# A four-stage attention, routing and expert kernel on one core: the first loads and keys reordered, and the first late expert job's rows fetched and transposed earlier

## The chip, the core and the metric

The kernel runs on one core of a Trainium2 chip. The core has five engines with their own instruction queues: TensorE (PE, with its weight loads shown apart as PEld), VectorE (DVE), ScalarE (ACT), GpSimd (POOL) and SyncE (SP, which here only issues DMAs). They are tied together by semaphores. The metric is the device time of one execution in microseconds (us). Before the change three runs took 1174.27, 1172.83 and 1172.62 us, median 1172.83. One further execution was profiled; all durations in this document that come from a trace come from such a profiled execution.

## The reference

Input `x` has 8 batches of 512 tokens of 256 numbers; a context of 64 rows per batch is attended to. All in 32-bit floats.

```
x = x + attention0(layernorm(x), ctx, ctx)        # 16 heads of 16, 64 keys per batch
x = x + ffn(layernorm(x))                         # in each batch the 75% of tokens
                                                  # with the highest score get gelu(x @ w_block)
x = x + attention1(layernorm(x), ctx, ctx, mask)
x = x + moe(x)                                    # 8 experts, the 2 best of each token, weights
                                                  # renormalised: silu(x@g) * (x@u) @ down, inner width 1024
```

The keys and values of both attentions depend only on the context and the weights, not on `x`. Which tokens go to which expert is known only once the third stage of all batches is done.

## The kernel before

**Two phases.** In the front phase (to about 545 us) the eight batches pass through both attentions, the feed-forward and the routing. The routing writes each token's row, 260 numbers wide with its token number, experts and weights behind the 256 features, into a DRAM buffer `xs` sorted by expert, with indirect scatters on GpSimd (L864). In the second phase the experts run as "jobs". A full job is 256 rows of one expert: fetch the rows, transpose them (4 matmuls against the identity), a gate-and-up product of 8 chunks of 8 matmuls each, the silu by ScalarE and two products on VectorE, 32 matmuls of outputs, a scaling by the routing weight on VectorE, and an indirect add of the rows to the output in DRAM on GpSimd (L106). Smaller jobs ("one", "pair") handle what is left over.

**Early and late jobs.** Seven full jobs (`NEARLY`) are early: they are put between the steps of the front phase as soon as half the batches are routed, with weights in buffers of their own (`e_wgu`, `e_wdn`). `early_steps(j)` gives their loads and their steps: `enter` (transposes L1159, copy L1162, token numbers and weights L1164 to L1176), four `gates` of two chunks each (matmuls L1183, activation L1191, products L1192 and L1193), and two `down` (matmuls L1210, scaling L1218, add). The other jobs follow in `order`, each with `load` (SP: two register loads, rows L1325, gate weights L1348, down weights L1354), `enter` (transposes L1365, copy L1367, token numbers and weights L1371 to L1385), `gate_up_full` (L1397, L1405, L1406) and `down` (L1454, L1462). A job's outputs are put behind the gates of the job after it. The first late job's list comes from `full_list`, on VectorE, which ends in writing `jobs`. Its rows may be fetched once the last scatter has landed (`routed`).

**Order.** Within an engine the order of the front phase is written out by hand in the string `ORDER`. Each letter takes the next step of one chain: a digit is a batch, A to H a batch's rank work, `k` keys, `v` values of one batch for both layers, `s` set-up steps sorted by a due time, `l` the two job lists, `j` early jobs. `in_order` ties the steps on PE, DVE, ACT and POOL to each other; SP's DMAs have no part in it and go in program order.

**The start.** SP, ScalarE and POOL issue the first loads in program order. `first_keys` makes layer 0's keys (L354) in two chunks and spreads each by ScalarE into a block-diagonal form `kbd` with a bias (L363, biased by `bkh`, which POOL makes at L349). `keys(1, c)` does the same for layer 1 on PE (L372) and VectorE (L380). `batch_values` makes one batch's values (L392), which VectorE biases and spreads into `vbd` (L401). A batch's attention is: statistics (L433 to L436), the reciprocal deviation `rstd` on POOL (L438), `shift` (L444), normalised rows `xn` (L447), transposes (L462) and copies (L465), queries (L494, L501), scores `sc` (L524), their maxima (L531, `pm` L539), scores the other way round and the exponentials (L547 to L564), context (L576), denominators `pz` (L591) and `bz` (L606), the product (L614), output projection (L625). The statistics step of batch 2 is in `ORDER` ahead of the shift step of batch 1.

Of the kernel before, what the change touches and what calls it, by code (L numbers as in the profile page):

```python
# [8 lines left out]
F32 = mybir.dt.float32  # L9
I32 = mybir.dt.int32  # L10
AF = mybir.ActivationFunctionType
# [4 lines left out]
P = 128  # L16
# [11 lines left out]
E = 8  # L28
# [19 lines left out]
NQ = P // QR  # L48

ORDER = """  # L50
sssssssssss0k0vvv0ss1020001s0k110s1s0s031010s7s2s403202410030v20120ss01040502A010A30A0As
101013010343201130005s12010sk0112151761Bs2B1BB112120241201v102s2050223s022302412C22123C2
C021C02131012110323150030sv024110331231041025231052000043313234260000D14D34Ds14D2341v233
613421632333442123454126154343114325134311114432E2524E1111544E452356E5472243423725234653
5264345645256352452222F36F35F63F222246455635547335546357453674356647435356733333556646v7
l63333476G464jj77j5jGj666j5j7jj47Gjjj765j7457j4G5j64654j7j6556747j5j7644644444j76sH6jj56
4444j557j76j7j57jj7Hsj76jjjjHH7565j65jj676jj7jj6j57j5j6j75557j5555jj7j6j667j55557jjjs67j
66j76j7676j66j76s66667j7jjjj7jj6666j77j7j7jjjjj77jjs7j7j7j7j7j777jj77jjjljj77jj77jj
"""


# [1 line left out]
def xattn_ffn_kernel(ctx: ExitStack, tc: tile.TileContext, a: dict, out: bass.AP):  # L63
# [53 lines left out]
    with ExitStack() as front:  # L117
# [49 lines left out]
        for t in range(TB):  # L167
            q = (nc.scalar, nc.scalar, nc.sync, nc.sync)[t]
            q.dma_start(x_sb[:, t, :], x_t[0][:, t, :])
        load_layer(0, ("wv", "wq"), nc.sync)  # L170
        nc.sync.dma_start(x_sb[:, TB : 2 * TB, :], x_t[1])
        load_layer(0, ("bo", "wo"), nc.sync)
        load_layer(1, ("wk", "bk"), nc.sync)
        for b in range(2, 4):
            nc.sync.dma_start(x_sb[:, b * TB : (b + 1) * TB, :], x_t[b])
        w_block = load_mat(nc.sync, "w_block")
# [55 lines left out]
        mhalf = const.tile([P, TB], F32, name="mhalf")  # L232
        setups.append((-0.9, lambda: nc.gpsimd.memset(mhalf, -0.5)))

        def loaded():
            load_layer(0, ("bk",), nc.gpsimd)
            load_layer(1, ("wv",), nc.gpsimd)

        setups.append((-0.862, loaded))

        def loaded():
            for l in range(2):
                load_layer(l, ("bv",), nc.gpsimd)
            load_layer(0, ("bq",), nc.gpsimd)

        setups.append((-0.855, loaded))

        ownh = within(
            -0.88, "ownh", [HC],
# [89 lines left out]
            layers[l]["vbd"] = vbd[:, l]  # L339
        setups.append((-0.93, lambda: nc.vector.memset(vbd[:, 0], 0.0)))  # L340
        setups.append((-0.858, lambda: nc.gpsimd.memset(vbd[:, 1], 0.0)))
        bkh = const.tile([P, 2, NC], F32, name="bkh")

        def first_keys():

            w = layers[0]
            two = [ps_m.tile([P, B, SK], F32, tag="m", name=f"ps_k_0_{c}") for c in range(NC)]
            for i in range(2):
                nc.gpsimd.tensor_scalar(  # L349
                    bkh[:, i, :], w["bk"], headm[:, i : i + 1], None, ALU.mult  # L350
                )
            for k in range(NC):
                for c in range(NC):
                    nc.tensor.matmul(  # L354
                        two[c],
                        lhsT=w["wk"][:, k, c * P : (c + 1) * P],
                        rhs=ctxT[:, k],
                        start=(k == 0),
                        stop=(k == NC - 1),
                    )  # L360
            for c in range(NC):
                for i in range(2):
                    nc.scalar.activation(  # L363
                        w["kbd"][:, c, :, i, :], two[c], AF.Identity,
                        bias=bkh[:, i, c : c + 1], scale=headm[:, i : i + 1],
                    )

        def keys(l, c):
            w = layers[l]
# [737 lines left out]
        e_xg = part_of_room(2, RW)  # L1107
        e_xT = part_of_room(NC, 2, P)
        e_sg = [part_of_room(1, 2 * P)]
        e_now = keep.tile([P, 2, D], F32, name="e_now")  # L1110
        e_w = {}
        piece = 2 * P

# [118 lines left out]
        for b in range(B):  # L1232
# [2 lines left out]
                attention_steps(b, 0, layers[0], False) + ffn  # L1235
                + attention_steps(b, 2, layers[1], True) + route_steps(b)
            )
        chains["k"] = [first_keys] + [lambda c=c: keys(1, c) for c in range(NC)]
        chains["v"] = [lambda b=b: batch_values(b) for b in range(B)]
        chains["s"] = [step for _, step in sorted(setups, key=lambda p: p[0])]  # L1240
        chains["l"] = [early_list, full_list]
        chains["j"] = early = []
        jobs_steps = [early_steps(j) for j in range(NEARLY)]
        early += jobs_steps[0][0]
        for j, (_, steps) in enumerate(jobs_steps):

            loads = list(jobs_steps[j + 1][0]) if j + 1 < NEARLY else []
            for n, step in enumerate(steps):
                early.append(step)
                if loads and n != len(steps) - 2:  # L1250
                    early.append(loads.pop(0))


        engines = (
# [46 lines left out]
    def kind(j):  # L1301
        return "full" if j < NLATE else "one" if j < NLATE + NONE else "pair"

    def load(j, late=False):
# [16 lines left out]
        xg = moe.tile([P, 2, RW], F32, tag="xg", name=f"xg_{j}", bufs=3)  # L1321

        def rows():
            for u, (row, _) in enumerate(at):
                i = nc.sync.dma_start(  # L1325
                    xg[u * size : u * size + size, 0:subs, :],
                    xs[bass.ds(row, subs * size), :].rearrange("(s p) w -> p s w", p=size),
                ).ins

                if what == "pair":  # L1330
                    after(i, tail_sent)
                else:
                    for other in tail_sent:
                        tc.declare_no_dep(i, other, reason="rows of tokens alone")
                    after(i, routed)

        if not late:
            rows()
# [12 lines left out]
        if late:  # L1351
            rows()
# [131 lines left out]
    assert sorted(order) == [j for j in range(NJOB) if j != spare]  # L1484

    def load_at(i):
        return load(order[i], i == 0) if i < len(order) else None

    loads = [load_at(0), load_at(1)]
    entered = []  # L1490
    in_order(lambda: entered.append(enter(order[0], loads[0][0])))

    def placed(i, step):

        if i < NPIN:
            got = []
            in_order(lambda: got.append(step()))
            return got[0]
        return step()

    pending = None
    for i, j in enumerate(order):
        w = loads.pop(0)[1]
        xT, tok, wt = entered.pop(0)
        if i > 0:
            loads.append(load_at(i + 2))
        if i == 0:

            hT = placed(i, lambda: gate_up_full(j, xT, w, None, range(NF // 2)))
            entered.append(placed(i, lambda: enter(order[1], loads[0][0])))  # L1510
            placed(i, lambda: gate_up_full(j, xT, w, hT, range(NF // 2, NF)))
        elif j < NLATE:
            hT = placed(i, lambda: gate_up_full(j, xT, w))
        else:
            h, hT = placed(i, lambda: gate_up_rows(j, xT, w))
        if i == 0:
            small_list()
            unit_list()
            loads.append(load_at(2))
        if 0 < i < len(order) - 1:  # L1520
            entered.append(placed(i, lambda: enter(order[i + 1], loads[0][0])))
        if pending is not None:
            placed(i, lambda: down(*pending))
        if j >= NLATE:
            placed(i, lambda: turn(j, h, hT))
        pending = (j, hT, w, tok, wt)
# [55 lines left out]
```

## Time and profile before

| | before |
|---|---|
| median of three runs | 1172.83 us |
| the profiled execution | 1164.97 us |
| its span, first to last instruction | 1163.3 us |
| TensorE clock granted in it | 0.999 |
| PE busy | 1144.1 us |
| DVE, ACT, POOL busy | 571.8, 375.7, 285.1 us |
| moved by DMA | 203.5 MB, mean 175 GB/s |

The span lies 1.7 us below the execution's own time; the profiled execution lies 7.9 us below the median of the runs. A line of the timeline gives the start (us from the span's start), the duration (of several instructions in a row together), engine, line of the kernel, operation, what it writes and reads, how many, and in brackets how long its engine was idle before it and which instruction ended that idle time. "SPq" is the queue that issues DMAs; the duration there is that of the issue, not of the transfer.

### The profile page before, as it was taken

The page shows a single profiled execution, that of the slowest core. Times are in us where ns is not written, and L with a number is a line of the kernel's source. Part 1 is how long each engine was busy: PE and PEld are TensorE (multiplying, and loading weights), DVE is VectorE, ACT ScalarE, POOL GpSimd, SP SyncE. Part 2 cuts the span into 40 slices and gives each one's busy share as a digit, 9 for nine tenths or more (in the row PEclk, how much of TensorE's full clock was granted, in tenths as well). Part 3 has the DMA queues.
Part 4 walks back from the last instruction along what each step waited for, and adds up shares of the span by engine and source line. Part 5 has one row for each costly group of instructions (what it writes and reads, how often), then busy time and mean ns, then how long its engine had stood idle before and what let it go on. Part 6 is the DMA issues. An engine that isn't in the chain of part 4 may idle for free. (4 is left out here: it accounts for less than half of the span.)

```text
span 1163.3 us, 20921 instructions
## 1 busy us (share of the span) xinstructions
PE 1144.1 (98%) x8016; PEld 823.8 (71%) x8016; DVE 571.8 (49%) x1660; ACT 375.7 (32%) x717; POOL 285.1 (25%) x312
## 2 busy tenths in 40 slices
PE   8999999999999999999999999999999999999997
PEld 4556666656667778778887776777767777667886
DVE  6798888898877766555722221222222221222221
ACT  4655655645544342322222112121121211211210
POOL 6330134233340512332411212112121121211112
PEclk9999999999999999999999999999999999999999
DMA  9000001010134444355889689997798977986711
GB/s 271 3 1 2 1 20 39 19 57 20 38 119 137 128 128 134 108 160 156 265 331 341 218 282 300 322 307 226 265 310 312 315 235 269 307 313 228 277 15 19
DMA packets 119589, 203.53 MB, mean 175 GB/s; under 512 B 10401, under 2 KB 105249, under 8 KB 107969
## 3 DMA queue, kind: packets, MB, share of 16 engines
q1 hardware_dynamic: 100048, 179.35, 44.0%
q0 software_dynamic: 14640, 18.12, 7.7%
q10 hardware_dynamic: 4800, 4.72, 1.2%
q8 instruction: 64, 1.05, 0.4%
q14 instruction: 37, 0.30, 0.1%
HBM read 180.38 MB, written 23.47 MB: 175 GB/s over the span
## 5 line engine op out<-in xcount | busy, mean ns | idle before, releaser
L1397 PE MATMUL gu<-xjT,wgu 128*128 128x256 f32 x1152 | 252.0, 379 | 0.7 <-ACT xjT L1367 0.7
L1397 PEld LDWEIGHTS gu<-xjT,wgu 128*128 128x128 f32 x1152 | 217.6, 190 | 31.0 <-issue 1.2
L106 POOL DMA_INDIRECT out_dram<-now,tok x63 | 98.1, 1557 | 475.7 <-DVE now L1462 287.1
L1454 PE MATMUL o<-wdn,hT 128*128 128x256 f32 (+1 forms) x1008 | 189.2, 380 | 0.0
L1454 PEld LDWEIGHTS o<-wdn,hT 128*128 128x128 f32 (+1 forms) x1008 | 151.1, 173 | 28.3 <-issue 1.7
L1406 DVE TENSOR_TENSOR hT<-sg,gu 128x256 f32<-128x256 f32 x144 | 60.6, 421 | 189.4 <-ACT sg L1405 189.2
L1405 ACT ACTIVATE sg<-gu 128x256 f32<-128x256 f32 x144 | 55.3, 384 | 208.5 <-PE gu L1397 207.1
L1424 PE MATMUL gr<-wgu,xjT 128*64 128x512 f32 (+1 forms) x432 | 120.8, 596 | 0.0
L1183 PE MATMUL gu_e<-x_sb,e_wgu 128*128 128x256 f32 x448 | 101.6, 382 | 0.6 <-ACT x_sb L1162 0.6
L1183 PEld LDWEIGHTS gu_e<-x_sb,e_wgu 128*128 128x128 f32 x448 | 83.8, 190 | 15.6 <-issue 2.2
L1462 DVE TENSOR_SCALAR now<-o,wt 128x256 f32<-128x256 f32 x53 | 25.6, 483 | 139.1 <-PE o L1454 139.0
L1424 PEld LDWEIGHTS gr<-wgu,xjT 128*64 128x64 f32 (+1 forms) x432 | 42.8, 150 | 68.4 <-issue 66.9
L864 POOL DMA_INDIRECT xs<-xr,slots x64 | 63.2, 988 | 104.7 <-issue 35.4
L438 POOL TENSOR_TENSOR rstd<-ve,mhalf 128x4 f32<-128x4 f32 x32 | 33.0, 1030 | 223.3 <-DVE ve L436 177.8
L531 DVE TENSOR_REDUCE mx<-sc 128x32 f32<-128x2048 f32 x32 | 73.2, 2288 | 14.9 <-PE sc L524 14.6
L1434 DVE TENSOR_TENSOR h<-sg,gr 128x512 f32<-128x512 f32 x34 | 23.4, 688 | 82.9 <-PE gr L1424 82.8
L494 PE MATMUL ps_q<-xT,w_wq 128*128 128x512 f32 x128 | 62.0, 612 | 0.5 <-ACT xT L465 0.5
L1433 ACT ACTIVATE sg<-gr 128x512 f32<-128x512 f32 x34 | 20.3, 597 | 124.7 <-PE gr L1424 124.7
L625 PE MATMUL py<-w_wo,cT 128*128 128x256 f32 x256 | 60.3, 384 | 0.0
L625 PEld LDWEIGHTS py<-w_wo,cT 128*128 128x128 f32 x256 | 47.3, 190 | 11.6 <-issue 5.3
L447 ACT ACTIVATE xn<-x_sb,shift,rstd 128x256 f32<-128x256 f32 x96 | 49.8, 594 | 11.6 <-DVE shift L444 11.5
L433 DVE BATCH_NORM_STATS2 st<-x_sb 128x6 f32<-128x256 f32 x128 | 51.3, 400 | 3.6 <-DMA x_sb<-in_x_dram 3.6
(295 smaller groups left out, 1452.9 us busy)
## 6 DMA issues: line engine op xcount, KB each, us to landing
wgu<-in_guT_dram SPq DMA_DIRECT2D x90, 1024.0 KB, 9.7
wdn<-in_dnT_dram SPq DMA_DIRECT2D x45, 1024.0 KB, 6.0
e_wgu<-in_guT_dram SPq DMA_DIRECT2D x56, 256.0 KB, 3.6
e_wdn<-in_dnT_dram SPq DMA_DIRECT2D x7, 1024.0 KB, 6.0
xg<-xs SPq DMA_DIRECT2D x18, 260.0 KB, 7.2
out_dram<-x_sb ACTq DMA_DIRECT2D x8, 512.0 KB, 4.6
x_sb<-in_x_dram SPq DMA_DIRECT2D x7, 512.0 KB, 8.2
x_sb<-xs SPq DMA_DIRECT2D x7, 260.0 KB, 2.8
```

Of the source, the lines that this page charges most:

```text
L106: i = nc.gpsimd.indirect_dma_start(out=out_rows, out_offset=bass.IndirectOffsetOnAxis(ap=tok, axis=0), in_=rows, in_offset=None, bounds_ch ...
L433: nc.vector.bn_stats(st, x_sb[:, b * TB + t, :])
L494: nc.tensor.matmul(ps, lhsT=w["wq"][:, k, c * P : (c + 1) * P], rhs=got["xT"][:, k, :], start=(k == 0), stop=(k == NC - 1),)
L531: nc.vector.tensor_reduce(got["mx"].rearrange("p t (r h) -> p r t h", r=NQ)[:, :, :, 2 * c : 2 * c + 2], sc, AX.X, ALU.max,)
L625: nc.tensor.matmul(py[:, s, :], lhsT=cT[:, c, t * P : (t + 1) * P], rhs=w["wo"][:, c, :], start=(c == 0), stop=(c == NC - 1),)
L864: i = nc.gpsimd.indirect_dma_start(out=xs, out_offset=bass.IndirectOffsetOnAxis(ap=slots[:, t, k : k + 1], axis=0), in_=xr[:, t, :], in_of ...
L1183: nc.tensor.matmul(ps[:, half, :], lhsT=e_w["gu"][:, c, o : o + P], rhs=e_xT[:, c].rearrange("p s q -> p (s q)"), start=(c == 0), stop=(c ...
L1397: nc.tensor.matmul(ps[:, half, :], lhsT=wgu[:, c, o : o + P], rhs=xT[:, c].rearrange("p s q -> p (s q)"), start=(c == 0), stop=(c == NC - 1),)
L1405: nc.scalar.activation(sg[:, 0 : 2 * P], ps[:, 0, :], AF.Silu)
L1406: nc.vector.tensor_tensor(hT[:, f, :], sg[:, 0 : 2 * P], ps[:, 1, :], ALU.mult)
L1424: nc.tensor.matmul(ps[rows], lhsT=xT[:, c, 0, rows], rhs=wgu[:, c, o : o + 4 * P], start=(c == 0), stop=(c == NC - 1),)
L1454: nc.tensor.matmul(ps[rows], lhsT=hT[:, f, s * P + rows.start : s * P + rows.stop], rhs=wdn[:, f, :], start=(f == 0), stop=(f == NF - 1),)
```

## The change

- **Loads at the start.** SP loads layer 1's key weights first, then layer 0's query weights, batch 1, and after it both layers' value weights. Before, layer 0's value and query weights came first, and layer 1's value weights went by POOL's queue. Layer 1's key bias goes from SP's queue to POOL's. POOL issues layer 0's key bias first of all, then its query bias and layer 1's key bias, and the value biases after the first `rstd`.
- **Keys and values at the start.** `bkh` becomes a set-up step of its own. ScalarE's two spreads of layer 0's keys become two steps (`first_taken`), of which the second stands behind batch 0's copies. Layer 1's first keys take the place of the first three value products, directly behind layer 0's keys; the three value products come after the queries of batch 1's first half, after the first `pz`, and ahead of a later transpose step.
- **The last early job (number 6).** Its `enter` is put ahead of early job 5's two `down`, and the loads of an early job are spread a little differently over the steps of the job before it. All eight last scatters come before job 5's adds. Before, four of them were between the gates of job 6.
- **The first late job.** Its rows are no longer fetched by SP behind its gate weights but by ScalarE's queue (`first_rows`), as part of the step of job 6's last gates but one: the instructions land between the activations of chunks 5 and 6. Its transposes, copy, token numbers and weights (`first_enter`) stand ahead of job 6's first `down`. They use room inside `x_sb` and PSUM tiles of the front phase.
- **The last job.** If it is a full one, the outputs of the job before it stand between the two halves of its gates rather than behind them.

```diff
 ORDER = """
-sssssssssss0k0vvv0ss1020001s0k110s1s0s031010s7s2s403202410030v20120ss01040502A010A30A0As
+ssssssssssss0k0k0sss10k20001s0110s1vs0s031010s7s2s40v320v2410030v20120ss01040502A010A30A
...
-        load_layer(0, ("wv", "wq"), nc.sync)
+        load_layer(1, ("wk",), nc.sync)
+        load_layer(0, ("wq",), nc.sync)
         nc.sync.dma_start(x_sb[:, TB : 2 * TB, :], x_t[1])
+        load_layer(0, ("wv",), nc.sync)
+        load_layer(1, ("wv",), nc.sync)
         load_layer(0, ("bo", "wo"), nc.sync)
-        load_layer(1, ("wk", "bk"), nc.sync)
...
+        setups.append((-0.97, lambda: load_layer(0, ("bk",), nc.gpsimd)))
+
         def loaded():
-            load_layer(0, ("bk",), nc.gpsimd)
-            load_layer(1, ("wv",), nc.gpsimd)
+            load_layer(0, ("bq",), nc.gpsimd)
+            load_layer(1, ("bk",), nc.gpsimd)
 
         setups.append((-0.862, loaded))
-
-        def loaded():
-            for l in range(2):
-                load_layer(l, ("bv",), nc.gpsimd)
-            load_layer(0, ("bq",), nc.gpsimd)
-
-        setups.append((-0.855, loaded))
+        setups.append((
+            -0.845, lambda: [load_layer(l, ("bv",), nc.gpsimd) for l in range(2)]
+        ))
...
+        def made():
+            for i in range(2):
+                nc.gpsimd.tensor_scalar(
+                    bkh[:, i, :], layers[0]["bk"], headm[:, i : i + 1], None, ALU.mult
+                )
+
+        setups.append((-0.857, made))
...
-            for c in range(NC):
-                for i in range(2):
-                    nc.scalar.activation(
-                        w["kbd"][:, c, :, i, :], two[c], AF.Identity,
-                        bias=bkh[:, i, c : c + 1], scale=headm[:, i : i + 1],
-                    )
+            first_two.extend(two)
+            first_taken(0)
+
+        def first_taken(c):
+            for i in range(2):
+                nc.scalar.activation(
+                    layers[0]["kbd"][:, c, :, i, :], first_two[c], AF.Identity,
+                    bias=bkh[:, i, c : c + 1], scale=headm[:, i : i + 1],
+                )
...
+        first_xT = part_of_room(NC, 2, P)
         e_now = keep.tile([P, 2, D], F32, name="e_now")
+        first_tok = keep.tile([P, 2], I32, name="first_tok")
+        first_wt = keep.tile([P, 2], F32, name="first_wt")
+
+        def first_rows():
+
+            row = nc.scalar.value_load(
+                jobs[0:1, 0, 0:1], min_val=0, max_val=E * QROWS + P - 2 * P
+            )
+            i = nc.scalar.dma_start(
+                e_xg, xs[bass.ds(row, 2 * P), :].rearrange("(s p) w -> p s w", p=P)
+            ).ins
+            for other in tail_sent:
+                apart(i, [other], "rows of tokens alone")
+            after(i, routed)
+
+        def first_enter():
+            ps = ps_m.tile([P, NC, 2, P], F32, tag="m", name="ps_e_first")
+            for c in range(NC):
+                for k in range(2):
+                    nc.tensor.transpose(ps[:, c, k, :], e_xg[:, k, c * P : (c + 1) * P], ident)
+            nc.scalar.copy(first_xT, ps)
+            nc.vector.tensor_copy(first_tok, e_xg[:, :, D].bitcast(I32))
...
-        chains["k"] = [first_keys] + [lambda c=c: keys(1, c) for c in range(NC)]
+        chains["k"] = [first_keys, lambda: keys(1, 0), lambda: first_taken(1), lambda: keys(1, 1)]
...
-        for j, (_, steps) in enumerate(jobs_steps):
-
-            loads = list(jobs_steps[j + 1][0]) if j + 1 < NEARLY else []
+        for j, (_, steps) in enumerate(jobs_steps[:-1]):
+
+            loads, steps = list(jobs_steps[j + 1][0]), list(steps)
+            if j == NEARLY - 2:
+
+                steps.insert(-2, jobs_steps[-1][1].pop(0))
             for n, step in enumerate(steps):
                 early.append(step)
-                if loads and n != len(steps) - 2:
+                if loads and (n < NF // 2 + 1 or n == len(steps) - 1):
                     early.append(loads.pop(0))
+        steps = jobs_steps[-1][1]
+
+        early += steps[:-3] + [lambda: (first_rows(), steps[-3]())]
+        early += [lambda: (first_enter(), steps[-2]()), steps[-1]]
...
-    entered = []
-    in_order(lambda: entered.append(enter(order[0], loads[0][0])))
+    entered = [(first_xT, first_tok, first_wt)]
...
+        elif i == len(order) - 1 and j < NLATE:
+
+            hT = gate_up_full(j, xT, w, None, range(NF // 2))
+            down(*pending)
+            pending = None
+            gate_up_full(j, xT, w, hT, range(NF // 2, NF))
         elif j < NLATE:
             hT = placed(i, lambda: gate_up_full(j, xT, w))
```

The rest of the diff takes the `late` argument and the first job's rows out of `load`, so that SP issues the first job's gate and down weights only, and renews the later rows of `ORDER`, in which the steps of jobs 5 and 6 and of the last scatters are reordered as told above.

More of the change, by code (lines that the diff above doesn't have):

```diff
@@ L50 @@
 ORDER = """
-sssssssssss0k0vvv0ss1020001s0k110s1s0s031010s7s2s403202410030v20120ss01040502A010A30A0As
[L52 to L58, printed above, removed]
+ssssssssssss0k0k0sss10k20001s0110s1vs0s031010s7s2s40v320v2410030v20120ss01040502A010A30A
+0As101013010343201130005s12010sk0112151761Bs2B1BB112120241201v102s2050223s022302412C2212
+3C2C021C02131012110323150030sv024110331231041025231052000043313234260000D14D34Ds14D2341v
+233613421632333442123454126154343114325134311114432E2524E1111544E452356E5472243423725234
+6535264345645256352452222F36F35F63F22224645563554733554635745367435664743535673333355664
+6v7l63333476G464jj77j5jGj666j5j7jj47Gjjj765j7457j4G5j64654j7j6556747j5j7644644444j76sH6j
+j564444j557j76j7j57jj7Hsj76jjjjHH7565j65jj676jj7jj6j57j5j6j75557j5555jj7j6j667j55557jjjs
+67j66j76j7676j66j76s66667j7jjjj7jj6666j77j7j7jjjjj77jjs7j7j7j7j7j777j77j7777jjjljjjjjj
 """
@@ L342, in xattn_ffn_kernel @@
         bkh = const.tile([P, 2, NC], F32, name="bkh")
+        first_two = []
+        def made():
[4 more added lines that the diff above has]
+        setups.append((-0.857, made))
         def first_keys():
@@ L347, in first_keys @@
             two = [ps_m.tile([P, B, SK], F32, tag="m", name=f"ps_k_0_{c}") for c in range(NC)]
-            for i in range(2):
-                nc.gpsimd.tensor_scalar(
-                    bkh[:, i, :], w["bk"], headm[:, i : i + 1], None, ALU.mult
-                )
             for k in range(NC):
@@ L360, in first_keys @@
                     )
-            for c in range(NC):
-                for i in range(2):
-                    nc.scalar.activation(
-                        w["kbd"][:, c, :, i, :], two[c], AF.Identity,
-                        bias=bkh[:, i, c : c + 1], scale=headm[:, i : i + 1],
-                    )
+            first_two.extend(two)
[6 more added lines that the diff above has]
+                )
         def keys(l, c):
@@ L1109, in xattn_ffn_kernel @@
         e_sg = [part_of_room(1, 2 * P)]
+        first_xT = part_of_room(NC, 2, P)
         e_now = keep.tile([P, 2, D], F32, name="e_now")
+        first_tok = keep.tile([P, 2], I32, name="first_tok")
[17 more added lines that the diff above has]
+            nc.vector.tensor_copy(first_tok, e_xg[:, :, D].bitcast(I32))
+            wt2 = small.tile([P, 2], F32, tag="wt2", name="wt2_first")
+            ej = job_e[:, 0:1]
+            nc.vector.scalar_tensor_tensor(
+                first_wt, e_xg[:, :, D + 1], ej, e_xg[:, :, D + 2], ALU.is_equal, ALU.mult
+            )
+            nc.vector.scalar_tensor_tensor(
+                wt2, e_xg[:, :, D + 1], ej, e_xg[:, :, D + 3], ALU.not_equal, ALU.mult
+            )
+            nc.vector.tensor_tensor(first_wt, first_wt, wt2, ALU.add)
         e_w = {}
@@ L1302, in kind, with load @@
         return "full" if j < NLATE else "one" if j < NLATE + NONE else "pair"
-    def load(j, late=False):
+    def load(j):
         what = kind(j)
@@ L1320, in load @@
             ]
[L1321 to L1338, printed above, removed]
+        xg = moe.tile([P, 2, RW], F32, tag="xg", name=f"xg_{j}", bufs=3) if j > 0 else None
+        for u, (row, _) in enumerate(at) if j > 0 else []:
+            i = nc.sync.dma_start(
+                xg[u * size : u * size + size, 0:subs, :],
+                xs[bass.ds(row, subs * size), :].rearrange("(s p) w -> p s w", p=size),
+            ).ins
+            if what == "pair":
+                after(i, tail_sent)
+            else:
+                for other in tail_sent:
+                    tc.declare_no_dep(i, other, reason="rows of tokens alone")
+                after(i, routed)
         w = []
@@ L1350, in load @@
                 )
-        if late:
-            rows()
         for (_, e), (_, wdn) in zip(at, w):
@@ L1486, in load_at @@
     def load_at(i):
-        return load(order[i], i == 0) if i < len(order) else None
+        return load(order[i]) if i < len(order) else None
     loads = [load_at(0), load_at(1)]
-    entered = []
-    in_order(lambda: entered.append(enter(order[0], loads[0][0])))
+    entered = [(first_xT, first_tok, first_wt)]
     def placed(i, step):
```

## The prediction

> **What bounds the kernel now.** I read the page's busy shares first, then the busy time by stretch, because a share of 98% says nothing of where the rest is. In the rows below the columns are the stretch, its length, and the busy time with the instruction count of PE, PEld, DVE, ACT and POOL, then the granted clock, the DMA share and GB/s.
>
> ```profile
> 12.00:24.00 12.00, 10.30 (x67) 5.39 (x68) 9.70 (x28) 7.88 (x15) 4.46 (x8) 1.00 0.98 290
> 24.00:45.00 21.00, 19.14 (x224) 11.06 (x223) 15.86 (x39) 14.69 (x25) 12.99 (x24) 1.00 0.26 75
> 45.00:540.00 495.00, 490.98 (x4715) 335.81 (x4714) 384.33 (x1074) 234.43 (x413) 142.04 (x179) 1.00 0.24 72
> ...
> 545.00:576.00 31.00, 29.32 (x138) 24.79 (x137) 25.55 (x128) 4.25 (x10) 14.25 (x12) 1.00 0.66 201
> 576.00:1140.00 564.00, 564.00 (x2753) 423.98 (x2752) 124.90 (x361) 109.50 (x245) 96.43 (x64) 1.00 0.79 271
> ```
>
> PE is idle for 19.2 us of the span (1163.3 - 1144.1). About 7.5 of them follow its last matmul (1155.8). From 576 on it never waits, so whatever is won or lost before 576 passes to the end undiminished; from 45 to 540 it waits 4.0 us in 495, too little to absorb a shift. The change acts on two places where PE does wait, the start (to 45) and the hand-over from the early jobs to the late ones (545 to 576). I therefore read the timeline of both. First the start:
>
> ```profile
> 18.90 0.43 DVE L433 BATCH_NORM_STATS2 st<-x_sb 128x6 f32<-128x256 f32 x1 [1.07 <-DMA x_sb<-in_x_dram]
> ...
> 21.24 0.16 DVE L444 SCALAR_TENSOR_TENSOR shift<-mv,rstd 128x4 f32<-128x4 f32 x1
> ...
> 24.31 1.17 PE L524 MATMUL sc<-kbd,qT 32*128 32x128 f32 x32
> ...
> 27.95 0.66 PE L539 MATMUL pm<-ident,mx 128*128 128x128 f32 x4 [0.55 <-DVE mx L531]
> ...
> 41.86 1.17 PE L524 MATMUL sc<-kbd,qT 32*128 32x128 f32 x32 [0.82 <-DVE cT L614]
> ```
>
> To be seen: DVE stands still for 1.07 us until batch 2's input lands at 18.9, runs batch 2's statistics (2.3 us) and only then batch 1's shift. Everything of batch 1 hangs on that shift. Now the hand-over:
>
> ```profile
> 551.49 14.22 PE L1183 MATMUL gu_e<-x_sb,e_wgu 128*128 128x256 f32 x64 [0.61 <-ACT x_sb L1162]
> ...
> 559.45 0.98 POOL L864 DMA_INDIRECT xs<-xr,slots  x1 [1.28 <-ACT x_sb L1191]
> ...
> 564.29 0.39 ACT L1191 ACTIVATE x_sb<-gu_e 128x256 f32<-128x256 f32 x1 [1.00 <-DVE r_b_o L1028]
> ...
> 565.55 7.43 PE L1210 MATMUL o_e<-e_wdn,x_sb 128*128 128x256 f32 x32
> ...
> 570.19 0.39 SPq L1325 DMA_DIRECT2D xg<-xs  x1
> ...
> 573.29 0.63 PE L1365 MATMUL ps_x<-ident,xg 128*128 128x128 f32 x4 [0.31 <-DMA xg<-xs]
> ...
> 574.59 7.17 PE L1397 MATMUL gu<-xjT,wgu 128*128 128x256 f32 x32 [0.68 <-ACT xjT L1367]
> ```
>
> To be seen: between the gates of early job 6 and the first late gate lie 9.04 us (565.55 to 574.59), nearly all of it outputs. The row fetch (3.0 us from 570.19) lies under those outputs; only 0.31 us of it shows.
>
> **Part A, the start.** Removed from before 13.1 us: three value products, 3 x 1.08 = 3.24 us of PE (L392), and on DVE their three pairs at 2 x 0.42 (L401). They come back after the first maxima transpose (pm) is near: one ahead of pm, one behind the first denominators, one ahead of the fourth transpose. Two things become earlier: layer 1's first keys (L372, 1.98 us) fill the place, and ScalarE has only one key pair (2 x 0.70) ahead of the normalised rows, not two. So the rows (13.21 now) can begin near 10.4, when the shift (10.23 + 0.16) is there: 2.8 us sooner, and the first scores near 17.2.
>
> That head start is then lost. In the new order DVE still has batch 2's statistics ahead of batch 1's shift. The bytes in front of batch 2's input are the same: 2944 KB on SP's queue, 512 on ScalarE's and about 530 on POOL's before, 3200, 512 and about 270 after. I leave its landing at 18.9, the shift at 21.24, and the second scores at 24.31. PE waits where it had the values to do. The layer-1 key bias pair on DVE (1.52 us at 24.18), now earlier, ended 0.1 us after the scores it stood beside: nothing. Behind that PE is the bound. Ahead of pm one value product has 0.55 us of idle to go into and costs 1.08 - 0.55 = 0.5. The other two (2.16) meet idle of 0.32 (at 39.73) and 0.82 (at 41.86), and DVE's product before 41.86 shifts with them in part: 2.16 - 1.14 = 1.0, less about 0.1. **A = +1.4**. If the input lands d earlier, A is 1.4 - d: if the later 1.14 of idle moves along by half, since DVE's own work shifts too, A is about 2.0, so 2.2 bounds it above; below, with the whole head start kept, 1.4 - 2.8 = -1.4. I allow 0.6 to 2.2 for the likely case.
>
> POOL's and SP's reordered issues (columns first, bias rows after the first rstd) change landings of a few us of loads whose users come later; the one exposed is the first key bias, now ahead of rstd on POOL. If it lands late, rstd is late, but the lost 2.8 us stand in front as cover. Priced at nothing, +1 if the cover is gone.
>
> **Part B, early job 6 enters ahead of job 5's outputs.** The 0.61 us wait for its copy (551.49) is covered by outputs. But four gates on, PE waits 0.27 us (558.54) for PSUM, held by DVE, which runs the late-list arithmetic from 551.53 to 557.6 with no gate in between. DVE's list starts no sooner, so PE meets the same gate: the wait grows by what was saved. All eight scatters now run back to back on POOL at about 1.3 us from 549.43: the last leaves near 558.5 rather than 567.75. **B = -0.1**; the gates end at 565.45.
>
> **Part C, the first late job's rows.** SP no longer stands before the down weights; that only moves loads earlier. New on ScalarE, between activations 5 and 6 of job 6: a register load and a DMA, waiting for the last scatter. New on PE: the four transposes (0.63) stand between gates and outputs, where nothing can pass them: outputs (32 matmuls, 6.95 bare: 7.43 less its 0.49 stall), then first late gates all queue behind the rows. Ideal, with the rows there: 0.63 + 6.95 + 0.6 (the first late gate then waits for DVE's last early output to leave PSUM, 0.48 and its hop) = 8.18, against 9.04: -0.86. To that comes the stall s until the rows land.
>
> ScalarE is free at 564.29 + 0.39 = 564.7. The register load is not in the trace on ScalarE; two on SP took 1.4 us (list ready 557.67, first load 559.09), so 0.7: the DMA leaves at 565.4, when the gates end. Its landing is then all exposed. The nearest rows:
>
> ```profile
> xg<-xs SPq DMA_DIRECT2D x18, 260.0 KB, 7.2
> ...
> out_dram<-x_sb ACTq DMA_DIRECT2D x8, 512.0 KB, 4.6
> ...
> x_sb<-xs SPq DMA_DIRECT2D x7, 260.0 KB, 2.8
> ```
>
> Here a rule of the Trainium skill speaks against the change: the page "DMA: Bandwidth & Descriptors", section "Issuing engines are not separate DMA queues", says that DMAs of scalar, sync and gpsimd run on the same 16 engines and interleave, and that another issuer saves only issue time. By the quiet row (2.8; 3.0 for the job's own fetch at 570.19, when the weights had landed) s would be 565.4 + 3.0 - 565.45 = 2.95 and C = +2.1. By the rule the fetch shares with 3 MB that SP has queued since 559 (two 1024 KB gate halves and now the down weights, 7 to 8 us at the 371 to 391 GB/s of that stretch), and with the next fetch and gates behind. ScalarE's output writes show that price: 4.6 us in the median, 5.7 and 5.8 where the DMA share was 1.01, so +1.2. I take 3.0 + 1.2 = 4.2: s = 4.15, **C = +3.3**. The ends: 2.95 (C = +2.1) and 6.0, the median of a transfer amid weight loads (page, wdn), with C = +5.1. Below zero it goes only if the fetch lands before 566.3, 0.9 us after it can leave; no row does that.
>
> **Part D, the tail.** The pending outputs go between the halves of the last gates. PE's work is the same and the last outputs, their add (1156.62) and its landing remain last: 0.
>
> **Sum.** 1.4 - 0.1 + 3.3 = +4.6 on the profiled 1164.97: 1169.6. The median of the runs, 1172.83, stands 7.9 above the profiled execution; I carry the difference: **1177.4**, with its own range 1175.3 to 1179.
>
> **Rivals.** (1) *The rows come in time to cost little and the start absorbs the values:* ScalarE fetches quickly (s = 1.5 to 2, by landing at 2 us like the 65 KB fetches) and the input lands 1 us earlier, since the bias rows no longer precede it on POOL. Then 0.4 - 0.1 + 0.9 = +1.2: 1174. For it: POOL's bytes; against: no 260 KB fetch under 2.8. (2) *Faster:* the head start of 2.8 us survives. It decides as soon as batch 2's input lands more than 1.4 us earlier (before 17.5); at 16.1 A = -1.4, and only if the stall at the rows is absent as well do B and C give -1.0: 1170.4. For it: SP's queue loses the small-packet bias column (1 KB) ahead of the input; against: equal bytes at a DMA share of 0.98. (3) *Worse:* the last scatter lands late. The two that left beside the gate load (559.45, 560.73) took 7.5 and 7.4 us, so the last, near 558.5, lands at 566, and the rows leave at 566.2 and take 6: s = 6.7, C = +5.9, sum +7.2: 1180. (4) *The order is not kept:* both orders are fixed per engine, so I give it nothing.
>
> **How the numbers follow.** The forecast 0.48, rival 1 0.20, rival 2 0.10, rival 3 0.22. What a measurement can tell from no change is 0.2%, 2.35 us: 1170.5 to 1175.2. Rival 1 is "same", rival 2 about at the lower bound (faster), the forecast and rival 3 slower. The range takes rival 1's upper half and rival 3's middle: 1173 to 1181.
>
> **What would show it.** Right: DVE's wait for batch 2's input grows while the shift stays near 21.2; pm near 28.5; an idle of PE of 3 us or more before the new transposes (L1140), released by the rows' DMA; the first late gate near 579; PE without idle after it. Wrong: the shift of batch 1 before 20, or a rows' DMA that leaves before 564, or transposes that follow the gates without a gap.

## The result: slower, and beyond the range

| | before | after |
|---|---|---|
| median (runs) | 1173.26 us (6) | 1185.47 us (6) |
| the profiled execution | 1164.97 us | 1184.87 us |
| its span | 1163.3 us | 1183.2 us |
| mean granted TensorE clock in it | 0.999 | 0.993 |
| PE busy | 1144.1 us | 1150.2 us |

The ratio is 1.0103, interval 1.009 to 1.0116: 12.2 us slower by the medians, where +4.6 was forecast. The two profiled executions differ by 19.9 us. That is not the change alone: the first profiled execution of before was 8 us quicker than its own runs, which experiment 1 takes up.

The busy time by stretch of the changed kernel first, the columns as in the prediction (stretch, length, busy time and count of PE, PEld, DVE, ACT and POOL, then clock, DMA share, GB/s):

```profile
24.00:45.00 21.00, 20.86 (x219) 12.08 (x218) 17.38 (x43) 13.70 (x23) 10.94 (x20) 1.00 0.18 47
45.00:540.00 495.00, 487.97 (x4687) 332.89 (x4686) 379.25 (x1056) 233.12 (x411) 142.09 (x179) 1.00 0.23 70
...
545.00:576.00 31.00, 26.31 (x120) 21.73 (x120) 24.03 (x115) 4.82 (x13) 11.13 (x10) 0.99 0.59 191
576.00:600.00 24.00, 15.80 (x61) 13.35 (x62) 6.25 (x30) 2.64 (x4) 7.98 (x7) 0.72 0.67 220
```

Three things are to be seen. From 24 to 45 PE is now fuller (20.86 against 19.14). From 45 to 540, where the order of the work is the same in both kernels, it is idle 3 us more. And from 545 to 600 it stands still for 12.9 us (before: 1.7), with a clock of 0.72 in the last row. The start in the timeline:

```profile
16.72 0.43 DVE L442 BATCH_NORM_STATS2 st<-x_sb 128x6 f32<-128x256 f32 x1 [2.28 <-DMA x_sb<-in_x_dram]
...
19.05 0.15 DVE L453 SCALAR_TENSOR_TENSOR shift<-mv,rstd 128x4 f32<-128x4 f32 x1
...
19.90 0.33 PE L471 MATMUL ps_x<-ident,xn 128*128 128x128 f32 x1 [1.60 <-ACT xn L456]
...
22.07 1.17 PE L533 MATMUL sc<-kbd,qT 32*128 32x128 f32 x32
...
26.11 0.66 PE L548 MATMUL pm<-ident,mx 128*128 128x128 f32 x4
```

The input of batch 2 lands 2.2 us earlier (16.72, was 18.90), the shift follows at 19.05 (21.24), the second scores at 22.07 (24.31), and the maxima's transpose starts at 26.11 (27.95). From 45 to 190 us everything stands 1.34 us earlier. The hand-over:

```profile
564.00 0.97 POOL L873 DMA_INDIRECT xs<-xr,slots  x1 [0.30 <-issue]
...
567.10 1.44 SPq L1391 DMA_DIRECT2D wgu<-in_guT_dram  x2
...
569.26 0.36 SPq L1395 DMA_DIRECT2D wdn<-in_dnT_dram  x1
...
571.28 0.39 SPq L1371 DMA_DIRECT2D xg<-xs  x1
...
571.87 1.79 SPq L1391 DMA_DIRECT2D wgu<-in_guT_dram  x2
...
573.51 0.41 ACTq L1129 DMA_DIRECT2D x_sb<-xs  x1
...
583.47 1.09 PE L1140 MATMUL ps_e_first<-ident,x_sb 128*128 128x128 f32 x4 [10.74 <-DMA x_sb<-xs]
...
584.34 9.55 PE L1251 MATMUL o_e<-e_wdn,x_sb 128*128 128x256 f32 x32
...
594.62 7.14 PE L1438 MATMUL gu<-x_sb,wgu 128*128 128x256 f32 x32 [0.73 <-issue]
```

The rows leave at 573.51, after SP has put out 3 MB for the first late job and is putting out the second job's; they land 9.8 us later, and PE stands still for 10.74 us. The outputs behind the stall take 9.55 us, where they took 7.43 (0.49 of it a wait). The trace's record of the granted clock has half the rate from 575.69 to 589.34, that is from 3 us into the stall until 5.9 us after it.

The trace's DMA packets show where the 9.8 us go. The rows are 272 packets, most of 1040 bytes. None of them moves before 577.2, while 1.2 MB of SP's loads do. By 579.1 all but 29 have passed, and these take until 582.9, one by one between SP's packets, most of which are the next gate weights' of 8 KB.

The 19.9 us between the two profiles are, in order of time: the start -1.34; 190 to 543 us, +6.78; to the end of job 6's gates, +1.58; from there to the first late gate, +13.01 (21.89 against 8.88); the last job, -0.10. The forecast had +1.4, nothing, -0.1, +3.3 and 0.

### The profile page after: what moved, and what is told of

The parts are those of the page before. It is cut to its first block, busy times and chain, and to the rows that moved or that the text cites. A ratio compares the mean times of both kernels' runs of the same rounds, so it can differ in the third digit from the quotient of the medians.

```text
span 1183.2 us, 20934 instructions
## 1 busy us (share of the span) xinstructions
PE 1150.2 (97%) x8016; PEld 827.6 (70%) x8016; DVE 572.4 (48%) x1660; ACT 375.2 (32%) x717; POOL 285.9 (24%) x312
## 5 line engine op out<-in xcount | busy, mean ns | idle before, releaser
L1438 PE MATMUL gu<-xjT,wgu 128*128 128x256 f32 x1088 | 238.1, 379 | 0.0
L1438 PEld LDWEIGHTS gu<-xjT,wgu 128*128 128x128 f32 x1088 | 205.6, 190 | 28.5 <-issue 1.2
L106 POOL DMA_INDIRECT out_dram<-now,tok x61 | 95.3, 1562 | 450.5 <-DVE now L1503 313.2
```

The costliest lines, as they stand in the source:

```text
L106: i = nc.gpsimd.indirect_dma_start(out=out_rows, out_offset=bass.IndirectOffsetOnAxis(ap=tok, axis=0), in_=rows, in_offset=None, bounds_ch ...
L1438: nc.tensor.matmul(ps[:, half, :], lhsT=wgu[:, c, o : o + P], rhs=xT[:, c].rearrange("p s q -> p (s q)"), start=(c == 0), stop=(c == NC - 1),)
```

## The experiments

The groups of runs were on different occasions, and the kernel before took 1173.5, 1166.5, 1172.9 and 1166.2 us in them. Only ratios within a group are compared. "Hand-over" below is the time from the end of job 6's last gate matmul to the first late gate, in the one profile of each kernel; "gates" is the time of job 6's 64 gate matmuls.

| kernel | ratio to before (interval) | gates | hand-over | half clock in the hand-over |
|---|---|---|---|---|
| before, first profile | | 14.22 | 8.88 | no |
| e1, before again | (one execution) | 14.21 | 8.96 | no |
| after | 1.0103 (1.009 to 1.0116) | 16.03 | 21.89 | 13.65 us |
| e9, after again | 1.0082 (1.0061 to 1.0102) | 15.48 | 17.35 | 6.8 us |
| e2, start alone | 0.9989 (0.9979 to 0.9999) | 14.24 | 9.14 | no |
| e11, start alone again | 0.9985 (0.9976 to 0.9994) | 14.21 | 9.04 | no |
| e3, hand-over alone | 1.0104 (1.0086 to 1.0122) | 15.96 | 19.92 | 10.2 us |
| e4, transposes behind the outputs | 1.0035 (1.0021 to 1.005) | 16.24 | 11.07 | no |
| e5, SP held | 1.0025 (1.0015 to 1.0034) | 14.63 | 14.88 | 6.8 us |
| e6, PE kept busy | 1.0068 (1.0051 to 1.0085) | 14.63 | 18.44 | no |
| e7, fetch sooner | 1.0032 (1.0018 to 1.0045) | 14.62 | 16.09 | 6.8 us |
| e8, part B alone | 0.9999 (0.999 to 1.0008) | 14.62 | 8.25 | no |
| e10, start and a fill that waited | 0.9999 (0.9988 to 1.001) | 14.23 | 9.14 | no |
| e12, repair with that fill | 1.0012 (1.0003 to 1.002) | 15.49 | 9.74 | no |
| e13, start and the right fill | 0.9982 (0.9975 to 0.9989) | 14.22 | 8.97 | no |
| e14, repair with the right fill | 0.9979 (0.9972 to 0.9986) | 14.60 | 12.02 | 3.4 us |

### 1. The kernel before, profiled again

No edit.

> The kernel before, unchanged, for a second trace. The profiled execution shown first took 1164.97 us, its unprofiled runs 1173. If the 6.8 us that the changed kernel's trace loses between 190 and 545 us at places whose order is the same belong to any execution and not to the change, this trace shows some 5 to 8 us of such losses too, at about 1171 to 1173 us in all. If they belong to the change, this trace repeats the first one: 1165 us, the early jobs' last outputs again at 543.

It took 1172.41 us, span 1170.6. The busy time of one stretch, 190 to 350 us, for the first profile of before, this one and the changed kernel:

```profile
190.00:350.00 160.00, 157.86 (x1824) 99.83 (x1817) 138.20 (x381) 85.57 (x144) 51.31 (x57) 1.00 0.15 50
```

```profile
190.00:350.00 160.00, 154.15 (x1753) 97.23 (x1750) 133.28 (x371) 83.06 (x140) 49.91 (x56) 1.00 0.13 42
```

```profile
190.00:350.00 160.00, 154.22 (x1777) 97.69 (x1768) 133.42 (x366) 84.34 (x142) 50.16 (x56) 1.00 0.13 42
```

The second and third have the same PE time and the first has 3.7 us more. Followed instruction by instruction, this execution of before falls back 7.3 us between 190 and 545, at the same places as the changed kernel (6.8). So that part of the difference is present in both kernels and comes with the occasion, and the change's own loss is what the medians say, 12 us. Against this second trace of before, the changed kernel's span is 12.6 us longer, and its hand-over 12.9. What makes the occasion stays open. The expectation of e9 below lays it to the chip, but the record gives the first and the fourth group the same chip number, with 1173.5 and 1166.2 us.

### 2. The two edits apart

The start alone takes the loads, the chain of keys and the first 57 steps of `ORDER` from the changed kernel; the hand-over alone takes the rest, without the last job.

> The start edit alone (loads, keys, values, first part of the order), the hand-over as before. Theory: the input of batch 2 lands 2.2 us earlier, so batch 1's shift follows earlier, and the start gains 1.3 us: ratio 0.999, about 1172. Rival (the prediction's part A): the values cost 1.4 us: 1174.7. In the trace batch 2's statistics start near 16.7.

> The hand-over edit alone (last early job, first late job's rows by ScalarE's queue, transposes ahead of the outputs), start and last job as before. Theory: all of the loss is here, +13 us: 1186, with a PE stall of about 10 us ahead of the new transposes, released by the rows' DMA, and half the TensorE clock after it. Rival (the prediction's part C): +3.3, a stall of 4 us at full clock: 1176.5.

The start alone gains 0.0011, and 0.0015 in e11, which is 1.3 to 1.8 us. The hand-over alone has the whole loss, with a stall of 10.24 us:

```profile
583.18 1.09 PE L1131 MATMUL ps_e_first<-ident,x_sb 128*128 128x128 f32 x4 [10.24 <-DMA x_sb<-xs]
```

The prediction's part A has the wrong sign. But the runs of the start alone lie between 1169.9 and 1175.6 us, and with them their mean clock, 0.999 to 0.994. The profile of e2 is its slowest run. This is the idle time ahead of batch 1's transposes, and the stretch behind it:

```profile
19.94 0.33 PE L471 MATMUL ps_x<-ident,xn 128*128 128x128 f32 x1 [1.68 <-ACT xn L456]
```

```profile
20.00:28.00 8.00, 7.76 (x46) 4.40 (x48) 4.23 (x2) 2.54 (x5) 6.68 (x13) 0.57 0.91 270
```

The column after POOL is the clock: 0.57. Its record has half the clock from 20.5 to 27.3, right behind PE's 1.68 us of idle, which began at 18.3 (and once more for 3.4 us from 252.6). In that run PE is 1.5 us later than before at 45 us, not 1.3 earlier.

### 3. The transposes behind the outputs

```diff
-        early += [lambda: (first_enter(), steps[-2]()), steps[-1]]
+        early += [steps[-2], lambda: (steps[-1](), first_enter())]
```

> The changed kernel with one move: the first late job's transposes, copy and weights stand behind job 6's outputs; the rows still come by ScalarE's queue at the same place. Theory: 7 of the 10.7 us of waiting are covered by outputs and the clock is not lowered, so 10 us come back: about 1175.5, stall about 3 to 4 us. Rival (the DMA itself, by its traffic, delays the late weights too, or the clock falls for another reason): under 5 us come back, 1180 or more.

8 of the 12 us come back, where 10 were expected. The longest waits of PE from 560 to 600 us (waiting line and tile, releaser, us in total, times, longest):

```profile
PE ps_e_first L1140 <- DMA x_sb<-xs: 1.6, 1, 1.6
PE gu_e L1224 <- DVE left L1042: 1.4, 1, 1.4
PE o_e L1251 <- DVE x_sb L1234: 0.8, 1, 0.8
```

The rows still take 9 us (issued at 576.71, transposes at 585.91), but 7 of them lie under outputs, and the stall is 1.6 us at full clock. Two smaller costs come into view: job 6's gates (1.4) and outputs (0.8) wait for VectorE.

### 4. The rows' landing, the clock, and the moment of the fetch

In the first run SP's queue waits for the rows before it puts out the down weights and all behind them:

```diff
             i = nc.sync.dma_start(wdn, dn_t[bass.ds(e, 1), :, :, :].rearrange("e p f o -> (e p) f o"))
+            if j == 0:
+                after(i.ins, first_sent)
```

with `first_sent` holding the rows' DMA.

> The changed kernel, and SP's queue waits for the first late job's rows to land before it issues that job's down weights and everything behind (the gate weights, 2 MB, still go ahead). Theory: the rows took 9.8 us because they share the engines with the 4 MB that SP had issued in the 4 us around them; alone they take 3 to 4 us, the stall of PE falls from 10.7 to about 4 us, the clock is not lowered or briefly, and 8 to 10 us come back: 1176. Rival (the rows are slow by themselves, from ScalarE's queue or after the scatters): they still take over 7 us, and 1183 or more.

The fetch, and PE's wait for it:

```profile
566.86 0.41 ACTq L1131 DMA_DIRECT2D x_sb<-xs  x1
...
570.86 1.09 PE L1143 MATMUL ps_e_first<-ident,x_sb 128*128 128x128 f32 x4 [3.80 <-DMA x_sb<-xs]
```

The rows land in 3.9 us and PE waits 3.80. In the same group, with SP not held, they take 6.5 us (e6) and 6.7 us (e7). So the loads that SP puts out behind them make them slower. Yet not the whole loss comes back: even this stall is followed by half the clock, as the stretches show:

```profile
567.00:571.00 4.00, 0.20 (x2) 0.17 (x2) 3.29 (x14) 0.77 (x2) 0.00 (x0) 0.85 0.78 207
571.00:582.00 11.00, 10.27 (x37) 8.42 (x37) 4.10 (x24) 0.59 (x1) 3.13 (x3) 0.75 0.93 330
```

PE stops at 567.1, the clock is halved at 569.8, 2.7 us later, and stays so until 576.6; the outputs take 9.47 us.

In the second run PE is kept busy during the stall:

```diff
             ps = ps_m.tile([P, NC, 2, P], F32, tag="m", name="ps_e_first")
+            for n in range(24):
+                nc.tensor.matmul(
+                    ps[:, 0].rearrange("p s q -> p (s q)"), lhsT=ident,
+                    rhs=e_w["gu"][:, 0, 0 : 2 * P], start=True, stop=True,
+                )
```

> The changed kernel with 24 matmuls of no use (128x256, about 0.22 to 0.38 us each, 5 to 9 us) ahead of the new transposes, into the same PSUM tile, which the transposes then write over. Theory: the half clock after the stall (13.65 us from 575.7, of which 5.9 us fell on work) follows from PE's standing still; with PE kept busy for most of the stall the outputs take 7 us again rather than 9.6, and about 3 us come back: 1182.5. Rival (the clock falls for another reason, the load of weights or a timer): no gain, 1185 or more.

```profile
563.12 0.41 ACTq L1129 DMA_DIRECT2D x_sb<-xs  x1
563.16 10.52 PE L1139 MATMUL ps_e_first<-e_wgu,ident 128*128 128x256 f32 x48
...
573.52 0.60 PE L1145 MATMUL ps_e_first<-ident,x_sb 128*128 128x128 f32 x4
573.96 7.07 PE L1256 MATMUL o_e<-e_wdn,x_sb 128*128 128x256 f32 x32
```

The program's 24 matmuls stand as 48 entries in the trace, as its other 32-bit matmuls do (not the transposes). The fill was too long: the rows had landed 6.5 us after 563.12, near 569.6, and 3.9 us of the fill are its own loss. But the clock is never halved, and the same 32 outputs take 7.07 us. With the rows and SP's loads as in the changed kernel, keeping PE at work was enough to keep the clock: in this hand-over the half rate came from PE's standing still. The four runs agree, with mean clocks of 0.997 and 0.998 (the changed kernel's six: 0.989 to 0.993).

The third run moves the fetch. `steps[-3]` is the step of job 6's last gates (not of its last but one, as the description of the change has it), and the fetch goes one step earlier:

```diff
-        early += steps[:-3] + [lambda: (first_rows(), steps[-3]())]
+        early += steps[:-4] + [lambda: (first_rows(), steps[-4]()), steps[-3]]
```

> The changed kernel with the rows' fetch one step earlier on ScalarE, between the activations of chunks 3 and 4 of job 6 rather than 5 and 6. Theory: the rows leave about 3 us earlier, ahead of SP's second job (its rows and gate weights are issued at 571.3 to 573.3), so they share with less: they land in 6 to 7 us, the stall is 5 to 6 us, 5 to 8 us come back: 1179. Rival 1 (only the moment counts): 3 us come back, 1182.5. Rival 2 (ScalarE waits for the last scatter with the activations of four chunks behind it): PE stalls in the gates instead, 1185 or more.

The rows left at 566.22, 1.2 us before the gates' end. The last scatter had been issued at 560.08, and SP's next fetch, which waits for that scatter too, left at 566.10: the scatter took about 6 us to land beside the gate weights. So the place on ScalarE was not the only bound; the fetch could not have gone much sooner. The stall was 5.63 us. The changed kernel was not in this group, so the ratios of e5, e6 and e7 show a direction, not an exact gain.

### 5. Part B alone

Job 6's `enter` and the eight scatters as in the changed kernel, the first late job's rows by SP and its transposes as before.

> Only the prediction's part B on the kernel before: job 6 enters ahead of job 5's outputs and all eight last scatters go ahead of job 5's adds; the first late job's rows and transposes as before. Prediction: -0.1. The traces of the changed kernel and of the hand-over edit alone show 1.7 us more from the end of job 5's gates to the end of job 6's, with VectorE and SP going in steps of 0.7 us near 565. Theory: that comes with part B: about 1175.2. Rival: it comes with the fetch by ScalarE: 1173.5.

The time does not change, as the prediction had it, and the +1.7 us of the expectation's theory did not come: gates 0.4 us longer, hand-over 0.6 shorter. But in its group e5 to e7 too have gates of only 14.6 us, while in groups one and three the kernels with the new hand-over have 15.5 to 16.2. Those are the groups with the losses of experiment 1, and in their traces SP too goes in steps of 0.7 us near 565: the changed kernel's gate weights leave 3.9 us after SP's first register load (563.17 to 567.10), against 1.4 before. The second job's loads then leave close to the rows' fetch. The cause of these steps stays open, and so does their share in the loss.

### 6. The change again, and the stall at the start filled

> The changed kernel once more, beside the others of this group. The second group ran on a chip where the kernel before takes 1166.5 us, 7 less than in the first group, and where its traces lack the losses between 190 and 545. Theory: those losses also shift SP's loads onto the rows' fetch, so without them the rows land in about 6.5 us, the stall is about 6.5 us and the clock is still lowered for some us: +8 us (ratio 1.007) on such a chip, +12 where the losses are there. Rival: +12 on any chip, so that the steps earlier or held bring 8 to 9 us as their ratios against before suggest.

> The start edit alone once more, beside the filled one: ratio 0.999, its runs spread by 5 us with the mean clock.

In e9 the ratio is 1.0082, a loss of 9.6 us, and its interval, 7.2 to 12 us, decides neither for +8 nor clearly against +12. The stall is 7.17 us: the rows took 6.3 us, without the late packets of the first trace, so even with the losses of experiment 1 the landing varies from trace to trace. What the change costs without those losses was not measured.

```diff
+        def filled():
+            ps = ps_m.tile([P, S], F32, tag="m", name="ps_fill")
+            for _ in range(3):
+                nc.tensor.matmul(
+                    ps[:, 0 : 2 * P], lhsT=ident, rhs=x_sb[:, 0, :], start=True, stop=True
+                )
```

The fill is a step of its own ahead of batch 1's first transposes.

> The start edit alone, and three matmuls of no use (128x256) in the 1.6 to 1.8 us in which PE stands still ahead of batch 1's first transposes. Runs of the start edit alone lie between 1169.9 and 1175.6 with mean clocks of 0.999 to 0.994: its slower trace has half the clock from 20.5 to 27.3, right after that idle. Theory: with the idle filled the clock stays up in all runs, and the kernel is 1 to 2 us faster than the start edit alone and 2.5 to 3.5 faster than before: ratio 0.9975. Rival (the clock falls for another reason): as the start edit alone, 0.999.

No gain, by a fault of the fill:

```profile
21.61 2.15 PE L1251 MATMUL ps_fill<-x_sb,ident 128*128 128x256 f32 x6 [3.10 <-POOL x_sb L493]
```

It read `x_sb`, to which POOL was adding the output bias, and so waited 3.1 us. The same fault is in e12, the repaired hand-over, which came out at 1.0012, not 0.9973:

```diff
-        early += [lambda: (first_enter(), steps[-2]()), steps[-1]]
+        early += [steps[-2], lambda: (first_enter(), steps[-1]())]
```

SP is held as in e5.

> The changed kernel repaired: SP waits for the rows before the down weights, the transposes stand between job 6's two outputs, and the idle at the start is filled. The rows have 3.5 us of outputs as cover and take 3.9, so PE waits about 0.5 us and the copy is covered by the second output. Theory: the hand-over is 0 to 0.5 us shorter than before, and with the start -3 us in all: ratio 0.9973. Rival (SP's held loads make late weights late): slower than before.

With `layers[0]["wq"][:, 0, :]` in place of `x_sb[:, 0, :]`:

> The start edit alone with three matmuls of no use, now on weights that nothing else waits for (in the fill before, they read x, which POOL was adding to, and so began at 21.6 and held PE back). They should begin at about 18.2 and end at 19.6, ahead of batch 1's first transposes at 19.9. Theory: the idle ahead of those transposes is what lowers the clock to half for 3.4 to 6.8 us in the slower runs of the start edit; filled, the mean clock stays at 0.997 or above in nearly all runs and the ratio to before is 0.9975 or less. Rival: the clock falls all the same, ratio 0.9985 as the start edit alone.

> The repaired hand-over (rows by ScalarE's queue, SP held, transposes between job 6's two outputs) with that same fill. In the first trace of it the outputs took 9.2 us with waits for VectorE's last products, since the fetch on ScalarE stands ahead of the last two activations. Theory: the hand-over is 0.8 us longer than before and its gates 1.2 us, so it is 2 us slower than the start edit with the fill: ratio 0.9995. Rival: with the right fill it is the fastest, 0.997.

The fill of e13 stands in the idle, and the clock of the stretch is full:

```profile
18.31 1.56 PE L1251 MATMUL ps_fill<-w_wq,ident 128*128 128x256 f32 x6
```

```profile
20.00:28.00 8.00, 7.67 (x71) 3.91 (x70) 5.72 (x8) 3.12 (x6) 6.08 (x12) 1.00 0.87 257
```

All 21 runs of e13 have a mean clock of 0.997 or more (before, in the same group: 0.995 or more) and lie within 3.7 us. By its ratio it is 2.1 us (1.3 to 2.9) faster than before (the medians are 1163.86 and 1166.22 us), a little less than the 0.9975 expected. That is the edit and the fill together. What the fill adds in time is not shown: the start alone was not in this group, and its ratios, 0.9989 and 0.9985, have intervals that overlap with that of e13. e14 is as fast (1163.54), so its rival is nearer than its theory, although the hand-over of its profile, its slowest run, is 12.02 us:

```profile
569.91 0.66 PE L1143 MATMUL ps_e_first<-ident,x_sb 128*128 128x128 f32 x4 [1.48 <-DMA x_sb<-xs]
570.41 5.31 PE L1254 MATMUL o_e<-e_wdn,x_sb 128*128 128x256 f32 x16
```

There half the clock follows a stall of only 1.48 us, and 16 outputs take 5.31 us rather than 3.5. The two best versions cannot be told apart; e13 has the plainer hand-over. In both, the fill does nothing but keep PE busy.

## Why the prediction was wrong, point by point

**What bounds it: right.** What was lost before 576 passed to the end undiminished: the shift between the traces is 19.99 to 20.00 us from 576 to 1067.

**Part A: wrong in sign.** The step that failed is "I leave its landing at 18.9". I counted the bytes in front of batch 2's input as equal and so its landing. It came at 16.72: d was 2.2, above the break-even of 1.4 that the text gave, which by its own formula makes -0.8; the trace shows -1.34. The shift before 20, named as a sign of being wrong, came (19.05). The value products did cost PE time behind the shift, but 0.9 us rather than 1.4: the lead falls from 2.24 at the second scores to 1.34 at 45 us.

The traces say in part why the input was early. SP issued it at 8.21 us, before at 9.77, behind the key bias column that rival 2 names (9.04). And at its landing SP's queue had moved 3.67 MB, before 3.86, where I had counted 3.20 and 2.94: loads issued behind the input move along with it, and the count left them out. Which of the reordered loads decided was not tried. Rival 2 had this half right.

**Part B: right** (-0.1 forecast, 0.9999 measured), but for the longer gates in some groups.

**Part C: right in its path, wrong in two terms.** The fetch leaves as the gates end (573.51 against a gates' end of 572.73), its landing is wholly exposed, and the transposes pass nothing. From the gates' end to the first late gate the sum has 4.15 of stall, 0.63 of transposes, 6.95 of outputs and 0.6 to the gate: 12.3 us. The trace has 10.74, 0.87, 9.55 and 0.73: 21.9.

The first term that failed is the landing. Set at 4.2 us, of which 1.2 for contention, it was 9.8 in the changed kernel and 9.4 in e3, 6.3 in e9, 6.5 in e6 and 6.7 in e7; all passed even the upper end of 6.0. I took ScalarE's output writes under load as the nearest row, but those met weights in pieces of 256 KB. The rows met gate weights, down weights, another fetch and the next gate weights. The median of the late jobs' own row fetches, the same transfer among such loads, was 7.2 us, and it stood in the first of the lines I showed (`xg<-xs`). Where SP was held the rows took 3.9 (e5), 4.1 (e12) and 5.6 us (e14), so the quiet price of 3.0 was not reached either.

The second is a term that the sum did not have: the clock behind the stall. Outputs and transposes took 2.8 us more than in the sum. The Trainium skill, "TensorE: Matmul & The Clock Gate", section "Part 1: The HAM clock gate (the "warmup" mystery)", says that the array falls to half its rate after an idle window of about 3.4 us. My own stall of 4.15 us should have called for it. The traces agree on the half rate and on the order of the time (2.7 and 3.0 us into the stall), and e6 shows that a busy PE keeps the clock. They differ on shorter stalls, some of which lowered it too (see the last section).

**Part D: right**, -0.10.

**Rivals.** Rival 3 named the late scatter. Its scatter held the fetch in e7 (6 us to land), but not in the changed kernel, where SP's fetch behind the same scatter left 2.2 us before ScalarE's. What would show the forecast right, "an idle of PE of 3 us or more before the new transposes", came, three times as long; "transposes that follow the gates without a gap" never did.

## What to carry to other kernels

Work that waits for a transfer goes behind the work that could cover it: here the same fetch costs 10.7 us ahead of 7 us of outputs and 1.6 behind them. A fetch on another engine's queue was no faster for it (6.5 us by SP in e8, 6.5 and 6.7 by ScalarE in e6 and e7), and what the other queue has put out, or will in the next microseconds, belongs in its price. And a long stall of TensorE was charged twice, once for itself and once for the work behind it at half the clock: all five stalls of 3.8 us and more in these hand-overs. A few matmuls of no use in the stall kept the clock in e6 and e13; that they pay for their place in time is not shown. They must read nothing that another engine is still writing (e10).

## What the runs showed of the hardware

- Half-clock periods came in lengths of 3.41, 6.83, 10.24 and 13.65 us, multiples of one length. The full-clock periods between them are multiples of it too: in each trace all changes of the clock lie on one grid of 3.41 us, and so the clock falls some time into a stall and returns some time after it.
- They followed every stall of 3.8 us or more in the hand-overs, but in some executions also stalls of 1.5 and 1.7 us (e14, e2), shorter than the 3.4 us of the page, and not in every execution: the changed kernel's profile has 1.60 us of idle at 18.3 and e4's a stall of 1.57, with a full clock behind them. In e2 the idle lies within one step of the grid and in the changed kernel across two, but e4's also lies within one, so the grid alone does not decide it.
- After the 10.7 us stall PE was at work again for 5.9 us before the clock came back; after the others 2.9 (e3), 3.9 (e9), 4.5 (e7) and 5.7 us (e5).
- The kernel before, unchanged, took 1166 or 1173 us by occasion. The 7 us lie between 190 and 545 us, at fixed places of the program where one engine goes on in steps of about 0.7 us without a wait that the profile shows. Both kernels have them.
